# A selective scan on one core: two groups' products in one instruction, the third group's scan first, preparation one round sooner

## The chip, the core and the metric

The kernel runs on one core of a Trainium2 chip. A core has a matrix engine (TensorE, PE), a vector engine (VectorE, DVE), a scalar engine (ScalarE, ACT) and GpSimd (POOL), each with its own instruction stream in order; all DMAs of the stretch treated here are issued from the queue of a fifth, SyncE (SP). The metric is the device time of one execution in microseconds. The kernel before takes 8124.83 us, the median of three runs (8120.56 to 8125.09).

## The reference, cut to what matters

Four layers on an input of 4 x 56 x 56 x 96. Layers 0 and 1 each contain a selective scan over L = 3136 positions, in four directions, for each of four images, with 192 channels and 16 states per channel:

```python
d_a = jnp.exp(dt[..., None] * a)                # decay per position, channel, state
d_b = dt[..., None] * b_ssm[:, :, None, :]
def step(h, inp):
    da_t, db_t, x_t, c_t = inp
    h = da_t * h + db_t * x_t[..., None]        # the recurrence
    y_t = jnp.einsum('bds,bs->bd', h, c_t)      # sum over the states
    return (h, y_t)
```

dt is softplus of a projection of the input u, B and C are projections too. Around the scans stand normalisations, projections, small convolutions and gates; layers 2 and 3 are linear attention and a quantised feed-forward part. All of that runs beside the scans, in "lanes".

## The kernel before

**Tiling.** The scans of both layers are one stream of chunks: layer, image, direction, and within a direction 7 chunks of CS = 448 positions, 2 x 4 x 4 x 7 = 224 chunks. A chunk has two channel halves e of 96 channels, and four quarters q of the 16 states: 8 rounds a chunk, 1792 rounds in all. A round works on 128 partitions (32 channels x 4 states) and three groups g of channels (NG = 3), each of 448 positions in the free dimension.

**A round n** (loop of `scans`, lines 690 to 774):

- `products` (719): DVE writes du * B into the state tile h, for groups 0 and 1 in one instruction each; du (dt * u, spread over the partitions) is in SBUF, B in the PSUM tile b, which PE makes by a selecting matmul (`spread_b`, 616).
- `begin(n + 1)` (714): POOL makes the product of group 2 for the next round; [...] B comes from the SBUF tile cb.
- `scan` (726): DVE runs the recurrence over each group in place, groups 0, 1, 2, with the decay from the PSUM tiles da0, da1, da2. After each scan ACT makes the decay of the next round for that group (`decay`, 678), an exponential of dt. There is one da tile per group, so decay, scan and next decay follow each other.
- `kept` (696) and `carried` (691): ACT copies the last column of h to `carry` and the carry of an earlier chunk into the h of round n + 2. The tiles h come from a ring of 3.
- hc (768): POOL multiplies h of all three groups by C, in one instruction of 1344 elements; two rounds later PE sums it over the states (`add_up`, 799).

**Preparation of a chunk** happens in rounds o before its first one (o = 0): input columns U (479), a projection on PE (448), its split into high and low parts (609, 587), dt's projection and softplus (496, 506, 508), dt * u on POOL (`times_u`, 521, one instruction for both halves e), both parked in DRAM (`park`, 526) and read back spread over the partitions (`spread`, 532: dt and du, two buffers each), B and C fetched in the same way (`fetch`, 550: cb, five buffers). dtc and duc, the tiles before parking, have one buffer each.

**Lanes.** In two slots of each round ("F" before, "C" after the first scan) pieces of the other layers' work are put into the streams of PE, ACT, DVE and POOL, if a running account of ACT and PE time (`spend`, `room`) has room. Line 697 enters the scans' own ACT time by the number r of the round in the chunk. `keep_busy` fills PE with matmuls on zeros (786). The convolutions in lanes read windows of the input from tiles win (958), from a ring of NWIN = 5.

**Order.** PE, ACT, DVE and POOL run exactly in the order written. The order of SP's DMAs is made by the tile framework's scheduler. A DMA whose buffer isn't free yet, or whose source isn't written, waits at the head of SP's queue, and those behind it wait too.

Of the kernel before, what the change touches and what calls it, by code (L numbers as in the profile page):

```python
# [11 lines left out]
F32 = mybir.dt.float32  # L12
# [4 lines left out]
ALU = mybir.AluOpType  # L17
# [3 lines left out]
HS = 56  # L21
L = HS * HS
C = 96
DI = 192
NS = 16
NE = 2
NG = 3
NQ = 4
# [4 lines left out]
CS = 448  # L33
ROW = CS + 2
WIDE = NG * ROW + 2
# [1 line left out]
NCS = L // CS  # L37
RANK = (12, 6)
NW, LATE_NW = 13, 20
NWIN = 5  # L40
OWN = ()
OWN_TAIL = ()

SPARE = (0.9, 2.4)
ACT_LIMIT, PE_LIMIT = 4.0, 7.0
# [122 lines left out]
class Net:  # L168
    def __init__(self, ctx, tc, aps, at, out):
# [5 lines left out]
        self.dram = pool("dram", bufs=1, space=bass.MemoryType.DRAM)  # L175
        self.nw, self.nwin, self.depth, self.banks, self.ring = NW, NWIN, DEPTH, BANKS, None
        self.tables = False
# [334 lines left out]
        t = self.sp.tile([rows, 2 + n * CS], F32, name=name, bufs=bufs)  # L512
        return t[:, 2:].rearrange("p (n t) -> p n t", t=CS)

    def times_u(self, ch):

        ch.duc = self.sp.tile([C, NE, CS], F32, name="duc", bufs=1)
        u = self.both.rearrange("p e (h w) -> p e w h" if ch.orient else "p e (h w) -> p e h w", w=HS)
        lo = ch.c * CS // HS
        in_rows = lambda t: t.rearrange("p e (a b) -> p e a b", b=HS)  # L520
        self.nc.gpsimd.tensor_tensor(in_rows(ch.duc), in_rows(ch.dtc), u[:, :, lo : lo + CS // HS], ALU.mult)  # L521

    def park(self, t):
        d = self.dram.tile([NE, 32, NG, CS], F32, tag="dd", name="dd", bufs=6)
        for g in range(NG):
            self.nc.sync.dma_start(d[:, :, g].rearrange("e d t -> d e t"), t[32 * g : 32 * g + 32])
        return d

    def spread(self, t, d):
# [25 lines left out]
    def prepare(self, ch, o):  # L555

        nc = self.nc
        if o == -14:  # L560
            self.parameters(ch)
        if o == (-14 if ch.opening else -12):
            self.inputs(ch)
        if o == -9:
            ch.cd = self.dram.tile([2 * NS, CS], F32, tag="cd", name="cd", bufs=3)
            nc.sync.dma_start(ch.cd, ch.cf[: 2 * NS])
        elif o == -5:
            self.times_u(ch)
            ch.dtd = self.park(ch.dtc)
        elif o == -4:  # L570
            ch.dud = self.park(ch.duc)
            self.spread_dt(ch, 0)
        elif o == -3:
            self.spread_du(ch, 0)
        elif o == 0:
            self.spread_du(ch, 1)
            self.spread_dt(ch, 1)
        if -3 <= o <= 0:
            self.fetch(ch, o + 3)

    def prepare_on_scalar(self, ch, o):

        if o == -10:
            self.rows(ch)
        elif o in (-9, -8):
            part = slice(64 if o == -9 else 96, 128)
            self.nc.scalar.copy(ch.cf[part], ch.ps[part])  # L587
        elif o in (-7, -6):
            self.softplus(ch, o + 7)

    def on_tensor(self, ch, o):

        for e in self.projected(ch, o):
            self.project_step(ch, e)
        if o in (-10, -9):
            self.less(ch, 64 if o == -10 else 96)
        elif o in (-8, -7):
            self.step_size(ch, o + 8)

    def projected(self, ch, o):  # L600

        return () if o not in (-12, -11) else (o + 12,) if not ch.first else (0, 1) if o == -11 else ()

    def less(self, ch, at):

# [17 lines left out]
    def scans(self):  # L623
# [7 lines left out]
        nc, sp = self.nc, self.sp  # L631
        chunks = []
        for l in range(2):
            for i in range(NB):
                for n, (orient, rev) in enumerate(ORDER[l]):
                    for step in range(NCS):
                        ch = Step()
# [9 lines left out]
        rounds = [(ch, e, q) for ch in chunks for e in range(NE) for q in range(NQ)]  # L647
# [7 lines left out]
        def steps(n):  # L655

            return [(ch, n - per * j) for j, ch in enumerate(chunks[max(0, n // per) : n // per + 3], max(0, n // per))]

        def ahead(n):
            for ch, o in steps(n):  # L660
                self.on_tensor(ch, o)

        for n in range(-14, 0):
            for ch, o in steps(n):
                self.prepare(ch, o)
            if n > -8:
                yield "F", n, 0
            for ch, o in steps(n):
                self.prepare_on_scalar(ch, o)
            ahead(n)  # L670
            if n > -8:
                yield "C", n, 0

        def decay(n, g):

            if n < len(rounds):
                ch, e, q = rounds[n]
                nc.scalar.activation(da[g][:, INNER], ch.dt[e][:, g], AF.Exp, scale=ch.par.na[:, e, q, g : g + 1])  # L678

        def column(t, at):  # L680

            return t[:, at : at + 2 * ROW + 1 : ROW]

        def carried(n):

            if n < len(rounds):
                ch, e, q = rounds[n]
                hs[n] = sp.tile([128, WIDE], F32, name="h", bufs=3)
                if not ch.step:
                    return  # L690
                nc.scalar.copy(column(hs[n], ROW if ch.rev else 1), ch.par.carry[:, e, q])  # L691

        def kept(n):
            ch, e, q = rounds[n]
            if ch.step < NCS - 1:
                nc.scalar.copy(ch.par.carry[:, e, q], column(hs[n], 2 if ch.rev else CS + 1))  # L696

        def own(n):
            ch, e, q = rounds[n]
            return NQ * e + q in (OWN_TAIL if ch.l and ch.i else OWN)  # L700

        hs, bs = {}, {}

        def tokens(t):

            return self.groups(t, 2)[:, :, :CS]

        def begin(n):

            if n < len(rounds):  # L710
                ch, e, q = rounds[n]
                bs[n] = self.spread_b(ch, q)
                if not own(n):
                    nc.gpsimd.tensor_tensor(tokens(hs[n])[:, 2], ch.du[e][:, 2], ch.cb[q][:, 1], ALU.mult)  # L714

        def products(n):
            ch, e, q = rounds[n]
            for g in range(3 if own(n) else 2):
                nc.vector.tensor_tensor(tokens(hs[n])[:, g], ch.du[e][:, g], bs[n], ALU.mult)  # L719

        def scan(n, g):
            ch, e, q = rounds[n]
            c = 1 if ch.step else 0
            way = slice(CS + 1 + c, 1, -1) if ch.rev else slice(2 - c, CS + 2)
            h = hs[n][:, g * ROW :]
            nc.vector.tensor_tensor_scan(h[:, way], da[g][:, way], h[:, way], 0.0, ALU.mult, ALU.add)  # L726

        carried(0)
        carried(1)
        begin(0)  # L730
        self.exp_and_ln()
        self.tables = True
        for g in range(NG):
# [2 lines left out]
        for n, (ch, e, q) in enumerate(rounds):  # L736
            r = NQ * e + q
            products(n)
            for c, o in steps(n):
                self.prepare(c, o)  # L740
            self.half_round()
            strided = [1.5 + 1.5 * ch.orient] * (r % NQ == 2)
            strided += [1.5 + 1.5 * c.orient for c, o in steps(n) for _ in self.projected(c, o)]
            self.spend((0.6, 0.7, 1.7, 0, 0, 0, 0.7, 0.6)[r], (1.3, 1.3, 0, 0, 0, 0, 0.4, 0.4)[r] + sum(strided))
            yield "F", n, r
            for c, o in steps(n):
                self.prepare_on_scalar(c, o)
            ended = late.pop(0) if len(late) == 2 else None
            if ended:
                self.keep_busy(ended[2])  # L750
            begin(n + 1)
            if ended:
                self.add_up(*ended)
            ahead(n)
            self.half_round()
            for g in range(NG):
                if g == 1:
                    yield "C", n, r
                if g == 2 and ended and ended[2] == NQ - 1:
                    self.spend(0.6, 0)  # L760
                    self.keep_sums(*ended[:3])
                scan(n, g)
                if g == 2:
                    kept(n)
                decay(n + 1, g)
            carried(n + 2)
            hc = sp.tile([128, NG, CS], F32, name="hc", bufs=3)
            nc.gpsimd.tensor_tensor(  # L768
                hc, tokens(hs[n]), ch.cb[q][:, 0].unsqueeze(1).to_broadcast([128, NG, CS]), ALU.mult,
            )  # L770
            late.append((ch, e, q, hc))
            del hs[n], bs[n]
# [659 lines left out]
```

## Time and profile before

| | us |
|---|---|
| median of the runs | 8124.83 |
| the profiled execution: its time | 8113.91 |
| its span in the trace | 8112.0 |
| scans, first product to last hc | 88 to 7903 |
| DVE busy | 7522.7 |
| POOL busy | 7167.9 |
| PE busy, filler on zeros included | 7168.4 |
| ACT busy | 6094.8 |

The costliest groups of the page (line, engine, operation, output<-inputs, size, count | busy time, mean ns of one | idle time of the engine just before them, and what ended most of it):

```profile
L726 DVE TENSOR_TENSOR_SCAN h<-da,h 128x449 f32<-128x449 f32 (+1 forms) x5376 | 5505.1, 1071 | 101.0 <-ACT da L678 84.0
L768 POOL TENSOR_TENSOR hc<-h,cb 128x1344 f32<-128x1344 f32 x1792 | 4883.1, 2725 | 615.1 <-DVE h L726 490.0
L678 ACT ACTIVATE da<-dt,na 128x448 f32<-128x448 f32 x5376 | 3353.6, 632 | 1109.4 <-DVE h L726 1087.3
L719 DVE TENSOR_TENSOR h<-du,b 128x448 f32<-128x448 f32 x3584 | 2015.8, 603 | 132.5 <-PE b L616 86.3
L714 POOL TENSOR_TENSOR h<-du,cb 128x448 f32<-128x448 f32 x1792 | 1753.5, 979 | 54.4 <-ACT h L691 29.8
L521 POOL TENSOR_TENSOR duc<-dtc,U 96x896 f32<-96x896 f32 x224 | 482.9, 2156 | 34.6 <-ACT dtc L508 34.6
```

Busy time counts overlapping instructions once, so count times mean is a little more than busy time: an instruction of DVE starts while the one before it still finishes.

### The profile page before, as it was taken

Reading aid. Unit: us, or ns where it says so; the run is one execution under the profiler, and the core shown is the slowest. Engines: PE = TensorE matmul, PEld = TensorE weight load, DVE = VectorE, ACT = ScalarE, POOL = GpSimd, SP = SyncE. Lnnn points to the kernel's source line nnn. Section 1 sums busy time; section 2 is a strip of 40 time slices with the busy share of each in tenths; the row PEclk is TensorE's granted clock in tenths of the full one; section 3 lists DMA queues with packets and bytes.
Section 4 is the critical chain, followed back from the end, with each engine's and each line's share of the span. In section 5 each row is a group of like instructions: output and inputs, shape, how many; then the busy total and the mean of one; then the engine's idle time right before and its main releaser. Section 6 shows DMA issues by size and latency. Waiting matters only on the chain.

```text
span 8112.0 us, 112271 instructions
## 1 busy us (share of the span) xinstructions
PE 7168.4 (88%) x33189; PEld 2503.7 (31%) x33189; DVE 7522.7 (93%) x9600; ACT 6094.8 (75%) x12759; POOL 7167.9 (88%) x3989
## 2 busy tenths in 40 slices
PE   7889888889888988889889889998899988999887
PEld 3233233222332223322232223333233322433233
DVE  6999999999999999999999999999989999899982
ACT  6778878786778767886677866787767877678776
POOL 5999999999999999999989998899988999789980
PEclk8889989899998988999889998889988898898987
DMA  5555665567556666566555665555655556555552
GB/s 177 180 185 188 198 193 183 174 198 222 182 179 193 208 196 188 178 201 193 189 180 180 197 220 176 174 162 169 195 178 164 168 174 195 167 164 166 173 163 66
DMA packets 568235, 1467.46 MB, mean 181 GB/s; under 512 B 108034, under 2 KB 337156, under 8 KB 566756
## 3 DMA queue, kind: packets, MB, share of 16 engines
q1 hardware_dynamic: 566848, 1458.49, 57.3%
q8 instruction: 261, 4.28, 0.2%
q14 instruction: 354, 2.90, 0.1%
q10 hardware_dynamic: 772, 1.80, 0.1%
HBM read 1186.49 MB, written 273.47 MB: 180 GB/s over the span
## 4 chain that ended last, share of the span: by engine, by line
PE 34%; DVE 30%; ACT 16%; issue 12%; POOL 4%; DMA 2%; SPq 0%; DVEq 0%; POOLq 0%; ACTq 0%
DVE h L726 22%; PE y L799 7%; DVE h L719 7%; PE y L786 5%; ACT da L678 5%; PE y L795 4%; PE b L616 3%; POOL hc L768 2%; PE pp L496 2%; ACT L830 2%; PE pp L448 2%; PE ps L875 1%; PE ps L947 1%; PE ps L860 1%; ACT Y L806 1%
## 5 line engine op out<-in xcount | busy, mean ns | idle before, releaser
L726 DVE TENSOR_TENSOR_SCAN h<-da,h 128x449 f32<-128x449 f32 (+1 forms) x5376 | 5505.1, 1071 | 101.0 <-ACT da L678 84.0
L768 POOL TENSOR_TENSOR hc<-h,cb 128x1344 f32<-128x1344 f32 x1792 | 4883.1, 2725 | 615.1 <-DVE h L726 490.0
L678 ACT ACTIVATE da<-dt,na 128x448 f32<-128x448 f32 x5376 | 3353.6, 632 | 1109.4 <-DVE h L726 1087.3
L719 DVE TENSOR_TENSOR h<-du,b 128x448 f32<-128x448 f32 x3584 | 2015.8, 603 | 132.5 <-PE b L616 86.3
L799 PE MATMUL y<-hc,four 128*32 128x448 f32 x14336 | 1918.2, 610 | 18.8 <-POOL hc L768 18.5
L714 POOL TENSOR_TENSOR h<-du,cb 128x448 f32<-128x448 f32 x1792 | 1753.5, 979 | 54.4 <-ACT h L691 29.8
L786 PE MATMUL y<-w,zeros 128*96 128x448 bf16 x5067 | 1415.0, 398 | 0.0
L616 PE MATMUL b<-cf,sel 128*128 128x448 bf16 x1792 | 679.1, 379 | 667.5 <-DVE h L719 661.1
L786 PEld LDWEIGHTS <-zeros 128*96 128x96 bf16 x5067 | 629.3, 135 | 1168.5 <-issue 1011.7
L448 PE MATMUL pp<-U,wd 96*128 96x448 f32 x896 | 666.6, 833 | 14.2 <-DMA U<-u 4.5
L799 PEld LDWEIGHTS y<-hc,four 128*32 128x32 f32 x14336 | 294.8, 113 | 1198.6 <-issue 681.3
L795 PE MATMUL y<-Y,ident 96*96 96x448 f32 x672 | 542.1, 896 | 37.8 <-ACT Y L806 19.8
L496 PE MATMUL pp<-cf,wd 12*96 12x448 f32 (+1 forms) x896 | 484.8, 623 | 89.9 <-ACT dtc L506 55.8
L521 POOL TENSOR_TENSOR duc<-dtc,U 96x896 f32<-96x896 f32 x224 | 482.9, 2156 | 34.6 <-ACT dtc L508 34.6
L696 ACT COPY carry<-h 128x3 f32<-128x3 f32 x1536 | 302.0, 197 | 260.6 <-DVE h L726 254.6
L806 ACT COPY Y<-y 96x448 f32<-96x448 f32 x448 | 342.1, 764 | 29.7 <-PE y L799 28.5
L691 ACT COPY h<-carry 128x3 f32<-128x3 f32 x1536 | 280.0, 182 | 51.3 <-POOL hc L768 48.4
L587 ACT COPY cf<-pp 64x448 f32<-64x448 f32 x448 | 235.6, 526 | 81.0 <-PE pp L609 72.7
L506 ACT ACTIVATE dtc<-pp,wd 96x448 f32<-96x448 f32 x448 | 281.6, 629 | 18.5 <-PE pp L496 14.0
L616 PEld LDWEIGHTS <-sel 128*128 128x128 bf16 x1792 | 184.9, 103 | 349.2 <-issue 280.7
L860 PEld LDWEIGHTS ps<-avg,w 96*112 96x112 f32 (+2 forms) x1936 | 246.2, 191 | 94.7 <-issue 58.4
L875 PEld LDWEIGHTS ps<-ident,rs 112*96 112x96 f32 x1744 | 217.3, 187 | 131.4 <-issue 89.4
(381 smaller groups left out, 5597.3 us busy)
## 6 DMA issues: line engine op xcount, KB each, us to landing
cb<-cd SPq DMA_DIRECT2D x896, 448.0 KB, 4.8
dt<-dd SPq DMA_DIRECT2D x448, 672.0 KB, 5.6
du<-dd SPq DMA_DIRECT2D x448, 672.0 KB, 5.8
dd<-dtc SPq DMA_DIRECT2D x672, 112.0 KB, 2.0
dd<-duc SPq DMA_DIRECT2D x672, 112.0 KB, 2.0
win<-m SPq DMA_DIRECT2D x252, 112.0 KB, 4.4
U<-u SPq DMA_DIRECT2D x112, 168.0 KB, 4.6
w<-z SPq DMA_DIRECT2D x84, 224.0 KB, 4.3
```

The costliest lines, as they stand in the source:

```text
L448: self.nc.tensor.matmul(ch.ps.rearrange("p (a b) -> p a b", b=HS), ch.par.wx[:, e], self.in_order(self.U[e], ch.orient, ch.c * CS, CS), st ...
L496: self.nc.tensor.matmul(ch.pd, ch.par.wt[rows, C * e : C * e + C], ch.cf[rows], start=True, stop=True)
L521: self.nc.gpsimd.tensor_tensor(in_rows(ch.duc), in_rows(ch.dtc), u[:, :, lo : lo + CS // HS], ALU.mult)
L616: self.nc.tensor.matmul(ps, self.sel[:, q], self.upper(ch.cf), start=True, stop=True)
L678: nc.scalar.activation(da[g][:, INNER], ch.dt[e][:, g], AF.Exp, scale=ch.par.na[:, e, q, g : g + 1])
L714: nc.gpsimd.tensor_tensor(tokens(hs[n])[:, 2], ch.du[e][:, 2], ch.cb[q][:, 1], ALU.mult)
L719: nc.vector.tensor_tensor(tokens(hs[n])[:, g], ch.du[e][:, g], bs[n], ALU.mult)
L726: nc.vector.tensor_tensor_scan(h[:, way], da[g][:, way], h[:, way], 0.0, ALU.mult, ALU.add)
L768: nc.gpsimd.tensor_tensor(hc, tokens(hs[n]), ch.cb[q][:, 0].unsqueeze(1).to_broadcast([128, NG, CS]), ALU.mult,)
L786: self.nc.tensor.matmul(self.y[:C], self.zeros[:, :C], self.some, start=False, stop=False)
L795: nc.tensor.matmul(o, w, self.in_order(a, ch.orient, ch.c * CS, CS), start=True, stop=False)
L799: nc.tensor.matmul(self.y[32 * n : 32 * n + 32], self.four, hc[:, g], start=n == 3, stop=n == 3 or q == NQ - 1,)
```

## The change

- `products` is one instruction for groups 0 and 1, with b repeated by a stride of zero.
- The scans of a round run in the order 2, 0, 1.
- POOL's product of group 2 (now `third`) is made for round n + 2; the h ring has 4 tiles, and `carried` serves round n + 3.
- Preparation runs one round sooner throughout; `times_u` is one instruction per half e, in rounds -6 and -5, after `third` in POOL's stream; parking is one DMA per half and group (12 a chunk for 6).
- U of a later pass is loaded at o = -13, after that round's `times_u`, instead of at -12.
- The ring of windows has 4 tiles (NWIN). The options OWN and OWN_TAIL, empty before, are gone.

```diff
-NWIN = 5
+NWIN = 4
...
-    def times_u(self, ch):
+    def times_u(self, ch, e):
...
+        in_rows = lambda t: t[:, e].rearrange("p (a b) -> p a b", b=HS)
+        u = self.in_order(self.U[e], ch.orient, ch.c * CS, CS)
+        self.nc.gpsimd.tensor_tensor(in_rows(ch.duc), in_rows(ch.dtc), u, ALU.mult)
...
-            self.nc.sync.dma_start(d[:, :, g].rearrange("e d t -> d e t"), t[32 * g : 32 * g + 32])
+            self.nc.sync.dma_start(d[e, :, g], t[32 * g : 32 * g + 32, e])
...
-        if o == -9:
+        elif o == -10:
             ch.cd = self.dram.tile([2 * NS, CS], F32, tag="cd", name="cd", bufs=3)
             nc.sync.dma_start(ch.cd, ch.cf[: 2 * NS])
+        elif o == -6:
+            ch.dtd = self.park(ch.dtc, 0)
+            self.park(ch.dtc, 1, ch.dtd)
         elif o == -5:
-            self.times_u(ch)
-            ch.dtd = self.park(ch.dtc)
+            ch.dud = self.park(ch.duc, 0)
+            self.spread_dt(ch, 0)
         elif o == -4:
-            ch.dud = self.park(ch.duc)
-            self.spread_dt(ch, 0)
-        elif o == -3:
+            self.park(ch.duc, 1, ch.dud)
             self.spread_du(ch, 0)
         elif o == 0:
             self.spread_du(ch, 1)
             self.spread_dt(ch, 1)
-        if -3 <= o <= 0:
-            self.fetch(ch, o + 3)
+        if -4 <= o < 0:
+            self.fetch(ch, o + 4)
...
+        def u_products(n):
+            for ch, o in steps(n):
+                self.prepare_on_gpsimd(ch, o)
+            for ch, o in steps(n):
+                if o == -13 and not ch.opening:
+                    self.inputs(ch)
...
-                hs[n] = sp.tile([128, WIDE], F32, name="h", bufs=3)
+                hs[n] = sp.tile([128, WIDE], F32, name="h", bufs=4)
...
+        def third(n):
+
+            if n < len(rounds):
+                ch, e, q = rounds[n]
+                nc.gpsimd.tensor_tensor(tokens(hs[n])[:, 2], ch.du[e][:, 2], ch.cb[q][:, 1], ALU.mult)
 
         def products(n):
             ch, e, q = rounds[n]
-            for g in range(3 if own(n) else 2):
-                nc.vector.tensor_tensor(tokens(hs[n])[:, g], ch.du[e][:, g], bs[n], ALU.mult)
+            b = bs[n].unsqueeze(1).to_broadcast([128, 2, CS])
+            nc.vector.tensor_tensor(tokens(hs[n])[:, :2], ch.du[e][:, :2], b, ALU.mult)
...
             begin(n + 1)
+            third(n + 2)
+            u_products(n)
...
-            for g in range(NG):
-                if g == 1:
+            for at, g in enumerate((2, 0, 1)):
+                if at == 1:
                     yield "C", n, r
...
-            carried(n + 2)
+            carried(n + 3)
```

More of the change, by code (lines that the diff above doesn't have):

```diff
@@ L39 @@
 NW, LATE_NW = 13, 20
-NWIN = 5
-OWN = ()
-OWN_TAIL = ()
+NWIN = 4
 SPARE = (0.9, 2.4)
@@ L513, in shifted, with park @@
         return t[:, 2:].rearrange("p (n t) -> p n t", t=CS)
-    def times_u(self, ch):
[L517 to L524, printed above, removed]
+    def times_u(self, ch, e):
+        if e == 0:
+            ch.duc = self.sp.tile([C, NE, CS], F32, name="duc", bufs=1)
+        in_rows = lambda t: t[:, e].rearrange("p (a b) -> p a b", b=HS)
+        u = self.in_order(self.U[e], ch.orient, ch.c * CS, CS)
+        self.nc.gpsimd.tensor_tensor(in_rows(ch.duc), in_rows(ch.dtc), u, ALU.mult)
+    def park(self, t, e, d=None):
+        if e == 0:
+            d = self.dram.tile([NE, 32, NG, CS], F32, tag="dd", name="dd", bufs=6)
         for g in range(NG):
-            self.nc.sync.dma_start(d[:, :, g].rearrange("e d t -> d e t"), t[32 * g : 32 * g + 32])
+            self.nc.sync.dma_start(d[e, :, g], t[32 * g : 32 * g + 32, e])
         return d
@@ L559, in prepare @@
         nc = self.nc
-        if o == -14:
+        if o == -15:
             self.parameters(ch)
-        if o == (-14 if ch.opening else -12):
-            self.inputs(ch)
-        if o == -9:
+            if ch.opening:
+                self.inputs(ch)
+        elif o == -10:
             ch.cd = self.dram.tile([2 * NS, CS], F32, tag="cd", name="cd", bufs=3)
             nc.sync.dma_start(ch.cd, ch.cf[: 2 * NS])
+        elif o == -6:
+            ch.dtd = self.park(ch.dtc, 0)
+            self.park(ch.dtc, 1, ch.dtd)
         elif o == -5:
-            self.times_u(ch)
-            ch.dtd = self.park(ch.dtc)
+            ch.dud = self.park(ch.duc, 0)
+            self.spread_dt(ch, 0)
         elif o == -4:
-            ch.dud = self.park(ch.duc)
-            self.spread_dt(ch, 0)
-        elif o == -3:
+            self.park(ch.duc, 1, ch.dud)
             self.spread_du(ch, 0)
@@ L577, in prepare, with prepare_on_gpsimd @@
             self.spread_dt(ch, 1)
-        if -3 <= o <= 0:
-            self.fetch(ch, o + 3)
+        if -4 <= o < 0:
+            self.fetch(ch, o + 4)
     def prepare_on_scalar(self, ch, o):
-        if o == -10:
+        if o == -11:
             self.rows(ch)
-        elif o in (-9, -8):
-            part = slice(64 if o == -9 else 96, 128)
+        elif o in (-10, -9):
+            part = slice(64 if o == -10 else 96, 128)
             self.nc.scalar.copy(ch.cf[part], ch.ps[part])
-        elif o in (-7, -6):
-            self.softplus(ch, o + 7)
+        elif o in (-8, -7):
+            self.softplus(ch, o + 8)
+    def prepare_on_gpsimd(self, ch, o):
+        if o in (-6, -5):
+            self.times_u(ch, o + 6)
     def on_tensor(self, ch, o):
@@ L594, in on_tensor @@
             self.project_step(ch, e)
[L595 to L598, printed above, removed]
+        if o in (-11, -10):
+            self.less(ch, 64 if o == -11 else 96)
+        elif o in (-9, -8):
+            self.step_size(ch, o + 9)
     def projected(self, ch, o):
-        return () if o not in (-12, -11) else (o + 12,) if not ch.first else (0, 1) if o == -11 else ()
+        return () if o not in (-13, -12) else (o + 13,) if not ch.first else (0, 1) if o == -12 else ()
     def less(self, ch, at):
@@ L657, in steps @@
             return [(ch, n - per * j) for j, ch in enumerate(chunks[max(0, n // per) : n // per + 3], max(0, n // per))]
+        def u_products(n):
[3 more added lines that the diff above has]
+                if o == -13 and not ch.opening:
+                    self.inputs(ch)
         def ahead(n):
@@ L661, in ahead @@
                 self.on_tensor(ch, o)
-        for n in range(-14, 0):
+        for n in range(-15, 0):
             for ch, o in steps(n):
@@ L696, in kept @@
                 nc.scalar.copy(ch.par.carry[:, e, q], column(hs[n], 2 if ch.rev else CS + 1))
-        def own(n):
-            ch, e, q = rounds[n]
-            return NQ * e + q in (OWN_TAIL if ch.l and ch.i else OWN)
         hs, bs = {}, {}
@@ L712, in begin @@
                 bs[n] = self.spread_b(ch, q)
-                if not own(n):
-                    nc.gpsimd.tensor_tensor(tokens(hs[n])[:, 2], ch.du[e][:, 2], ch.cb[q][:, 1], ALU.mult)
+        def third(n):
+            if n < len(rounds):
+                ch, e, q = rounds[n]
+                nc.gpsimd.tensor_tensor(tokens(hs[n])[:, 2], ch.du[e][:, 2], ch.cb[q][:, 1], ALU.mult)
         def products(n):
             ch, e, q = rounds[n]
-            for g in range(3 if own(n) else 2):
-                nc.vector.tensor_tensor(tokens(hs[n])[:, g], ch.du[e][:, g], bs[n], ALU.mult)
+            b = bs[n].unsqueeze(1).to_broadcast([128, 2, CS])
+            nc.vector.tensor_tensor(tokens(hs[n])[:, :2], ch.du[e][:, :2], b, ALU.mult)
         def scan(n, g):
@@ L726, in scan @@
             nc.vector.tensor_tensor_scan(h[:, way], da[g][:, way], h[:, way], 0.0, ALU.mult, ALU.add)
-        carried(0)
-        carried(1)
+        for n in range(NG):
+            carried(n)
         begin(0)
+        third(0)
+        third(1)
         self.exp_and_ln()
@@ L751, in scans @@
             begin(n + 1)
+            third(n + 2)
+            u_products(n)
             if ended:
@@ L755, in scans @@
             self.half_round()
-            for g in range(NG):
-                if g == 1:
+            for at, g in enumerate((2, 0, 1)):
+                if at == 1:
                     yield "C", n, r
-                if g == 2 and ended and ended[2] == NQ - 1:
+                if at == 2 and ended and ended[2] == NQ - 1:
                     self.spend(0.6, 0)
@@ L762, in scans @@
                 scan(n, g)
-                if g == 2:
+                if at == 2:
                     kept(n)
                 decay(n + 1, g)
-            carried(n + 2)
+            carried(n + 3)
             hc = sp.tile([128, NG, CS], F32, name="hc", bufs=3)
```

## The prediction

> **What bounds the kernel now.** I read the busy shares first, then the stretch of the scans alone, then the vector engine (DVE) in order of time, then its waits, then GpSimd (POOL) in order of time and the waits of the DMA queue (SP).
>
> The page's busy line and the scan stretch (columns of the second: stretch, length, then each engine's busy time and instructions, granted clock, DMA share, GB/s):
>
> ```profile
> PE 7168.4 (88%) x33189; PEld 2503.7 (31%) x33189; DVE 7522.7 (93%) x9600; ACT 6094.8 (75%) x12759; POOL 7167.9 (88%) x3989
> ...
> 88.00:7903.00 7815.00, 6940.13 (x32496) 2399.83 (x32496) 7446.10 (x9394) 5915.64 (x12424) 7136.68 (x3953) 0.90 0.59 184
> ```
>
> 1792 rounds take 7815 us, 4.36 us each. DVE is idle for 7815 - 7446 = 369 us of it. PE's share holds 1415 us of filler (line 786, zeros), so PE is less full than it looks. POOL is the close second: 7137 us.
>
> DVE in order of time, where no other work is mixed in (start, length, engine, line):
>
> ```profile
> 2070.12 1.12 DVE L719 TENSOR_TENSOR h<-du,b 128x448 f32<-128x448 f32 x2
> 2071.16 3.05 DVE L726 TENSOR_TENSOR_SCAN h<-da,h 128x449 f32<-128x449 f32 x3
> 2074.13 1.12 DVE L719 TENSOR_TENSOR h<-du,b 128x448 f32<-128x448 f32 x2
> 2075.18 3.05 DVE L726 TENSOR_TENSOR_SCAN h<-da,h 128x449 f32<-128x449 f32 x3
> 2078.14 1.12 DVE L719 TENSOR_TENSOR h<-du,b 128x448 f32<-128x448 f32 x2
> ```
>
> From start to start: two products 1.04 to 1.05 us, three scans 2.96 to 2.97, a round 4.01 without a gap. Counting round lengths in these DVE rows over the whole trace, 1130 of 1792 rounds are below 4.05 us: in almost two thirds DVE alone sets the pace. The others hold either work of the side lanes on DVE (some 450 instructions, about 220 us) or a wait. The waits of DVE in the scan stretch (us in total, times, longest):
>
> ```profile
> DVE h L719 <- PE b L616: 86.3, 94, 9.5
> DVE h L726 <- ACT da L678: 84.0, 167, 2.5
> DVE w L889 <- PE ps L875: 33.5, 19, 3.7
> ...
> DVE h L726 <- POOL h L714: 15.1, 15, 2.0
> ```
>
> They are scattered over PE, ACT and side lanes; POOL's product of the third group ends last only 15 times.
>
> POOL in order of time around the product dt*u (line 521):
>
> ```profile
> 3011.14 2.73 POOL L768 TENSOR_TENSOR hc<-h,cb 128x1344 f32<-128x1344 f32 x1 [4.70 <-DVE h L726]
> 3013.81 1.77 POOL L521 TENSOR_TENSOR duc<-dtc,U 96x896 f32<-96x896 f32 x1
> 3015.54 0.98 POOL L714 TENSOR_TENSOR h<-du,cb 128x448 f32<-128x448 f32 x1
> 3016.48 2.74 POOL L768 TENSOR_TENSOR hc<-h,cb 128x1344 f32<-128x1344 f32 x1
> 3019.17 0.98 POOL L714 TENSOR_TENSOR h<-du,cb 128x448 f32<-128x448 f32 x1
> 3020.10 2.74 POOL L768 TENSOR_TENSOR hc<-h,cb 128x1344 f32<-128x1344 f32 x1
> ```
>
> hc and the third product take 3.62 us a round (3016.48 to 3020.10), and every eighth round line 521 adds 1.73 us (1.76 to 2.59 long, by orientation). 8 x 3.62 + 2.15 = 31.1 us a chunk, against 8 x 4.01 = 32.1 on DVE.
>
> [...] the trace has 0.52 from product to product, [...] The trace's own check: a 97x97 product of the same kind (line 1330) lasts 230 ns and a 448 one 603, so 1.06 ns per element and about 0.13 us fixed, of which 0.08 overlaps the next instruction. The forecast goes by the trace's 0.52, [...]
>
> **The change part by part.**
>
> *Joint product.* Two instructions of 448 become one of 896 with b repeated. Estimate: [...], against 1.05: 0.057 us a round, 1792 x 0.057 = 102 us. No DVE row has a repeated PSUM operand. Bounds: 0.97 at best (saves 0.08, 143 us), 1.05 at worst (saves nothing); not longer, since the elements are the same. I take 0.99. Not all of it arrives: the waits view has some 430 waits, so about a quarter of the rounds end on PE, ACT or a lane; half of those I count as lost, leaving 88%: **-90 us**.
>
> *Scan of group 2 first.* Without it the scan of group 0 would follow directly on the joint product that feeds it. With it, a scan of 0.99 us stands between. Scan, decay on ACT and next scan of a group stay one round apart, with the same 2.4 us to spare (4.01 - 0.99 - 0.63). Zero.
>
> *Third product two rounds ahead, four h buffers.* Before, POOL has it done 3.6 us after the end of the previous round's scans, and it is needed at 7.0: 3.4 us to spare, 1.2 in the round with line 521. After, it is needed at 4 + 4 + 1.0 = 9.0: 5.4 to spare. The 15.1 us of waits for it nearly go: **-12 us**. What is late next on POOL is hc: its h buffer must be free before ACT copies the carry in at the round's end, hc ends 2.7 us into the round, so 1.3 us are to spare there, as before; the longer h ring moves carry and buffer together.
>
> *dt*u in halves over two rounds.* 448 instructions for 224. From POOL's rows, (2725 - 978) / 896 = 1.95 ns per element, so about 0.1 us fixed: 224 x 0.09 = 20 us more POOL time. It hides in POOL's idle time before hc (490 us on line 726), but that shrinks: +5 us. In return the lump behind which hc waits is about 1.1 us twice instead of 2.2 once.
>
> *Preparation a round sooner.* On PE and ACT it is the same work one round earlier. The table of ACT time kept free for it (by round number) is not moved, so lanes are put where softplus is: +5 us (0 to 15).
>
> *SP's queue.* Parking dt and dt*u now takes 12 DMAs a chunk instead of 6: 1344 more at 0.42 us of issue (1.26 for three), 560 us. The bytes stay. SP has that time:
>
> ```profile
> SPq L550 <- POOL hc L768: 1401.2, 598, 7.8
> SPq L526 <- ACT dtc L508: 1256.8, 209, 19.9
> SPq L526 <- POOL duc L521: 928.6, 217, 8.7
> ```
>
> But with five cb buffers, fetch of quarter q=1..3 a round sooner takes a buffer whose last reader, hc four rounds back, ends only 2.7 us into the issuing round. The POOL instruction that needs it comes two hc later, at least 7.2 us; landing is 4.8 (page's DMA part) and issue 0.4: 2.0 us to spare, where it was about 6. Zero, if nothing else blocks the queue.
>
> *U of the next pass* (seven times): loaded after the last half of dt*u, which ends 0.7 us into the next round, in which PE already wants it 2.8 us in; landing is 4.6 us. PE stands about 3 us; half reaches DVE: +10 us (0 to 28).
>
> *Four win buffers.* The third window of a convolution now takes the buffer that PE has just read; at the head of each of four images it is needed a round later, landing 4.4 plus issue 1.3: PE 2 to 3 us late: +8 us (0 to 13).
>
> *Opening.* One more round of prologue and every opening load a round sooner: +4 us (0 to 20).
>
> Sum: -90 - 12 + 5 + 5 + 10 + 8 + 4 = **-70 us**. The profiled execution has 8113.9 us (span 8112.0), so 8044; the median of the runs shown, 8124.8, lies 10.9 above it: **8055 us**, 0.86% faster. Range of this case: 8010 to 8095.
>
> **The rivals.**
>
> *POOL becomes the bound.* A vertical chunk needs 8 x 3.62 + 2.6 + 0.1 = 31.7 us there, DVE then 8 x 3.955 = 31.6. For it: the tie, and hc already starts late after line 521. Against: lanes and waits give DVE another 0.2 us a round. If half of the 90 us is lost, 8100.
>
> *The joint product saves nothing* (1.05 us): -12 + 32 remains, 8145. Against it speaks that the fixed part shows in every DVE row.
>
> *SP's queue makes it slower.* A fetch with 2.0 us to spare stands in one queue with stores that wait for ACT or DVE up to 10 us (the Y stores, line 811, 348 us in 59 waits). Where one is over 2 us late, POOL stops before the third product, and POOL has nearly no free time, so that time counts in full. It outweighs the gain from 70/224 = 0.3 us per chunk; at 0.7 us per chunk +157 - 70 gives 8210. Against: SP waits 2.3 us on average in front of fetches, so it is early, not late.
>
> **How the numbers follow.** Main case 0.62 (8055), POOL bound 0.13 (8100), nothing saved 0.07 (8145), SP queue 0.18 (8210). 0.2% is 16 us, about what a measurement can tell from no change. Faster: main case and three quarters of POOL, 0.70; slower: SP queue mostly and half of "nothing saved", 0.20; same 0.10. Low end: joint product at its best and all of it arriving, 8113.9 - 143 + 11 = 7982, little likely, so 7995; high end to the SP case: 8170.
>
> **What would show it.** Right: one DVE product a round with about 1.07 us length, the next scan 0.99 us after its start; undisturbed rounds at 3.95; no wait of a scan for POOL; hc waits for DVE fall clearly below 490 us. SP rival: POOL's third product waits for cb or du DMAs (17.4 us before) in the hundreds. POOL rival: ACT's copy of the carry waits for hc far above 48 us. The forecast is wrong if undisturbed rounds stay at 4.01, or if they reach 3.95 and DVE's idle time grows by over 70 us.

## The result: 0.5% slower, with the mechanism forecast in place

The changed kernel takes 8159.29 us (median, 8156.76 to 8169.87) against 8122.69 us before; the ratio is 1.0051, 95% interval 1.0033 to 1.0068. The forecast was 8055 us; the time lies inside the range given, but on the other side of no change. The profiled execution has 8156.8 us, span 8155.0, where before it had 8113.9 and 8112.0: 43 us more. Below, times of different runs are compared by their ratio to the kernel before, which ran beside each of them.

DVE in order of time, changed kernel (start, length, engine, line):

```profile
2102.02 1.06 DVE L732 TENSOR_TENSOR h<-du,b 128x896 f32<-128x896 f32 x1
2102.99 3.05 DVE L739 TENSOR_TENSOR_SCAN h<-da,h 128x449 f32<-128x449 f32 x3
2105.96 1.06 DVE L732 TENSOR_TENSOR h<-du,b 128x896 f32<-128x896 f32 x1
2106.94 3.05 DVE L739 TENSOR_TENSOR_SCAN h<-da,h 128x449 f32<-128x449 f32 x3
```

The joint product takes 0.98 us from its start to the scan's; an undisturbed round takes 3.94 to 3.95 us, against 4.01. That is what the forecast rested on. The stretch of the scans, and DVE's longest waits in it:

```profile
88.00:7938.00 7850.00, 6888.50 (x32415) 2377.43 (x32414) 7335.25 (x7596) 5903.99 (x12412) 7158.66 (x4173) 0.90 0.57 183
```

```profile
DVE h L739 <- ACT da L691: 171.5, 216, 3.1
DVE h L732 <- PE b L621: 142.3, 130, 13.1
DVE w L1099 <- PE ps L1097: 41.6, 19, 3.6
...
DVE h L739 <- POOL h L727: 1.0, 2, 0.5
```

DVE works 7335 us instead of 7446: 111 us saved. But it is idle 7850 - 7335 = 515 us instead of 369, 146 more. Waits for ACT's decay doubled (84.0 to 171.5), those for PE's b rose from 86.3 to 142.3, and a lane's step on line 1099 appears (41.6). The wait for POOL's third product is gone, as forecast.

Where the idle time lies is told by the round within the chunk (idle time ahead of DVE's instructions, summed from the trace over all chunks with the shortest gaps too, so a little above the 369 and 515; us):

| round r | 0 | 1 | 2 | 3 | 4 | 5 | 6 | 7 | sum |
|---|---|---|---|---|---|---|---|---|---|
| before | 66 | 30 | 47 | 82 | 67 | 7 | 22 | 56 | 377 |
| changed | 99 | 73 | 73 | 33 | 65 | 24 | 120 | 38 | 525 |

Round 3, where the double product dt*u used to stand in POOL's stream, became better by 49 us. Round 6 became worse by 98, rounds 0 to 2 together by 102. In those rounds ACT's preparation now stands: its first copy of the projection moved from round 6 to round 5, softplus from rounds 1 and 2 to 0 and 1. The copy of the finished sums (line 823) stays in rounds 1 and 5. And the table on line 759 (697 before), from which the lanes learn how much ACT time to leave free, still has 0 for round 5 and 0.7 for round 1, where the 1.6 us end of softplus now runs.

One such place, round 718 (r = 6): ACT, PE and DVE in order of time, changed kernel.

```profile
3200.92 1.28 ACT L921 ACT_TABLE_LOAD   x1
3202.22 0.64 ACT L921 ACTIVATE w<-ps,inb 128x448 f32<-128x448 f32 x1
3202.88 0.63 ACT L922 ACTIVATE w<-ps,inb 64x448 f32<-64x448 f32 x1
3203.51 1.28 ACT L847 ACT_TABLE_LOAD   x1
...
3205.31 0.63 ACT L487 ACTIVATE cf<-pp,cscale 128x448 f32<-128x448 f32 x1
3205.84 1.19 ACT L691 ACTIVATE da<-dt,na 128x448 f32<-128x448 f32 x2
3206.96 0.52 ACT L823 COPY Y<-y 96x448 f32<-96x448 f32 x1
```

```profile
3206.00 0.53 PE L614 MATMUL pp<-cf,minus 64*64 64x448 bf16 x1 [4.17 <-ACT cf L487]
3206.45 4.32 PE L1097 MATMUL ps<-w,w 128*96 128x448 f32 x6
```

```profile
3206.57 1.09 DVE L739 TENSOR_TENSOR_SCAN h<-da,h 128x449 f32<-128x449 f32 x1 [2.10 <-ACT da L691]
3210.82 0.68 DVE L1099 SCALAR_TENSOR_TENSOR w<-ps,c,w 96x448 f32<-96x448 f32 x1 [3.15 <-PE ps L1097]
```

A lane's piece with two table loads (ACT_TABLE_LOAD, 1.28 us each; 3.83 us of work from 3200.92 on) stands ahead of the copy cf (487) and of the decays. PE, in order, waits 4.17 us for cf; the lane's matmuls behind it come late; DVE waits 2.10 us for its decay and then 3.15 us for the lane's sum. One overfull round of ACT costs DVE 5.25 us.

This is one of the worst places, and the chunk being prepared opens a direction, which puts two more short instructions of ACT in the rows left out. But it is of the common kind. By a count in the traces, table loads start during round 5 in 37 of the 224 chunks, in both kernels. In the rounds that follow them (r = 6) DVE is idle for 10 us in the kernel before, and for 80 of round 6's 120 us in the changed one.

### The profile page after: what moved, and what is told of

The parts are those of the page before. It is cut to its first block, busy times and chain, and to the rows that moved or that the text cites. A ratio compares the mean times of both kernels' runs of the same rounds, so it can differ in the third digit from the quotient of the medians.

```text
span 8155.0 us, 110085 instructions
## 1 busy us (share of the span) xinstructions
PE 7126.6 (87%) x33155; PEld 2487.4 (31%) x33155; DVE 7421.3 (91%) x7811; ACT 6089.5 (75%) x12757; POOL 7198.6 (88%) x4213
## 4 chain that ended last, share of the span: by engine, by line
PE 30%; DVE 29%; ACT 16%; issue 15%; POOL 6%; DMA 4%; SPq 1%; DVEq 0%; POOLq 0%; ACTq 0%
DVE h L739 19%; DVE h L732 9%; PE y L816 6%; ACT da L691 4%; POOL hc L785 4%; PE y L803 3%; PE y L812 3%; PE pp L446 2%; PE pp L494 2%; ACT L847 2%; PE ps L877 2%; PE ps L892 2%; PE b L621 1%; PE ps L964 1%; DMA cb<-cd 1%
## 5 line engine op out<-in xcount | busy, mean ns | idle before, releaser
L739 DVE TENSOR_TENSOR_SCAN h<-da,h 128x449 f32<-128x449 f32 (+1 forms) x5376 | 5504.9, 1072 | 182.0 <-ACT da L691 171.5
L732 DVE TENSOR_TENSOR h<-du,b 128x896 f32<-128x896 f32 x1792 | 1904.4, 1063 | 144.5 <-PE b L621 142.3
L519 POOL TENSOR_TENSOR duc<-dtc,U 96x448 f32<-96x448 f32 x448 | 526.3, 1175 | 23.4 <-ACT dtc L506 23.4
L494 PE MATMUL pp<-cf,wd 12*96 12x448 f32 (+1 forms) x896 | 467.3, 602 | 68.8 <-ACT cf L587 37.9
L614 PE MATMUL pp<-cf,minus 64*64 64x448 bf16 x448 | 178.2, 398 | 144.5 <-ACT cf L487 82.5
```

The source lines that it names most:

```text
L494: self.nc.tensor.matmul(ch.pd, ch.par.wt[rows, C * e : C * e + C], ch.cf[rows], start=True, stop=True)
L732: nc.vector.tensor_tensor(tokens(hs[n])[:, :2], ch.du[e][:, :2], b, ALU.mult)
```

## The experiments

Three theories stood at first. 1: preparation meets the turnover of the sums (the rounds in which finished sums are copied out), with a table that doesn't know. 2: DVE's gain can't arrive, since PE, ACT or POOL are at their own limit. 3: POOL is late and holds ACT's carry.

### Preparation on ACT and PE back in its old rounds

```diff
-        if o == -11:
+        if o == -10:
             self.rows(ch)
-        elif o in (-10, -9):
+        elif o in (-9, -8):
...
-        elif o in (-8, -7):
-            self.softplus(ch, o + 8)
+        elif o in (-7, -6):
+            self.softplus(ch, o + 7)
...
-        elif o == -6:
+        elif o == -5:
             ch.dtd = self.park(ch.dtc, 0)
             self.park(ch.dtc, 1, ch.dtd)
-        elif o == -5:
             ch.dud = self.park(ch.duc, 0)
-            self.spread_dt(ch, 0)
```

(projection, split, step size, parameters and B, C to DRAM one round later too; dt spread at -4)

> The changed kernel, but ScalarE's and TensorE's part of the preparation (projection, its split, softplus) back in the rounds where the kernel before has it; dt*u stays in halves in rounds -6 and -5, the third product two rounds ahead. Theory 1 (the new waits come from preparation now meeting the turnover of the sums on ACT and PE, in rounds 1, 2, 5 and 6 of a chunk): idle time of DVE falls back to about 370 us and the 111 us of DVE time arrive, 8010 to 8060 us. Theory 2 (DVE's gain can't arrive, because PE, ACT or POOL are at their own limit): still 8110 or more, DVE idle above 450 us. Theory 3 (POOL late: hc, carry, next third product): about 8130, since POOL's order is as in the changed kernel.

Ratio 0.9968 (0.9957 to 0.9978): 0.83% below the changed kernel, of the sign that theory 1 expects, above its window. Round 6 falls back to 38 us of DVE's idle time, the sum is 477. The halves of dt*u now directly follow softplus, and POOL waits for it (one of these waits, of 26.2 us, lies outside the scans' steady part):

```profile
POOL duc L519 <- ACT dtc L506: 109.8, 53, 26.2
```

Round 3 has 102 us idle. So this run doesn't separate theory 1 cleanly; it put a wait of its own in.

### The joint product split again, in the changed kernel

```diff
-            b = bs[n].unsqueeze(1).to_broadcast([128, 2, CS])
-            nc.vector.tensor_tensor(tokens(hs[n])[:, :2], ch.du[e][:, :2], b, ALU.mult)
+            for g in range(2):
+                nc.vector.tensor_tensor(tokens(hs[n])[:, g], ch.du[e][:, g], bs[n], ALU.mult)
```

> The changed kernel with the joint product split again into two instructions of 448. Theory 1: the waits are new and apart from DVE's pace, so the 0.06 us a round come back nearly in full, 8235 to 8270 us. Theory 2: DVE's idle time takes most of it, 8160 to 8190, idle falling by 80 us or more. Theory 3: in between, since POOL gets 0.06 us a round more to catch up.

Ratio 1.0135 (1.012 to 1.015). Against 1.0051 the joint product is worth 0.84%, 68 us of the 111. The time lies between the windows of theories 1 and 2, and DVE's idle time is only about 35 us lower than with the joint product, so both have a part: three fifths arrive, and without the joint product the change would have cost 1.35%.

### The joint product alone, in the kernel before

```diff
-            for g in range(3 if own(n) else 2):
-                nc.vector.tensor_tensor(tokens(hs[n])[:, g], ch.du[e][:, g], bs[n], ALU.mult)
+            b = bs[n].unsqueeze(1).to_broadcast([128, 2, CS])
+            nc.vector.tensor_tensor(tokens(hs[n])[:, :2], ch.du[e][:, :2], b, ALU.mult)
```

> The kernel before with the joint product alone; scans stay in the order 0, 1, 2, so the scan of group 0 follows on the product that feeds it. If the order 2, 0, 1 matters, that scan starts only when the product is complete, about 0.1 us later than in the changed kernel (1.06 against 0.98), and the round stays at 4.01 to 4.05: 8110 to 8150. If it doesn't, undisturbed rounds fall to 3.95, and by theory 1 and 3 (preparation and POOL as before) the time is 8020 to 8050, by theory 2 8100 or more.

Ratio 1.0178 (1.0161 to 1.0195), slower than the case in which the order matters. DVE in order of time:

```profile
2092.48 1.06 DVE L719 TENSOR_TENSOR h<-du,b 128x896 f32<-128x896 f32 x1
2093.64 3.06 DVE L726 TENSOR_TENSOR_SCAN h<-da,h 128x449 f32<-128x449 f32 x3
2096.62 1.06 DVE L719 TENSOR_TENSOR h<-du,b 128x896 f32<-128x896 f32 x1
```

The scan that needs the product starts 1.16 us after it, not 0.98: 0.18 us a round, and the round is 4.14 us. It is so in all 1792 rounds: 1.156 us at the least, where the changed kernel has under 1.1 us in 1540. The order 2, 0, 1 is what makes the joint product pay, by far more than the forecast's "zero" suggests for it taken by itself.

### The tables moved with the preparation

```diff
-SPARE = (0.9, 2.4)
+SPARE = (0.95, 2.4)
...
-            self.spend((0.6, 0.7, 1.7, 0, 0, 0, 0.7, 0.6)[r], (1.3, 1.3, 0, 0, 0, 0, 0.4, 0.4)[r] + sum(strided))
+            self.spend((0.7, 1.7, 0, 0, 0, 0.7, 0.6, 0.6)[r], (1.3, 0, 0, 0, 0, 0.4, 0.4, 1.3)[r] + sum(strided))
```

> The changed kernel with the tables of ScalarE and TensorE time set aside by round number moved one round sooner, like the preparation itself; the spare time per half round is 0.95 instead of 0.9, without which the lanes don't end in time. Theory 1, if the stale table is the cause: DVE's waits for ACT in rounds 1, 2 and 6 fall and the time is 8070 to 8120. Theory 1, if the work itself collides there: 8140 to 8170. Theories 2 and 3: 8150 to 8170.

SPARE is the time of ACT and of PE, in us, by which the account's backlog falls each half round; a lane's piece goes in only if the backlog with it stays under a limit (ACT_LIMIT, PE_LIMIT).

Ratio 0.9914 (0.9895 to 0.9933), 8046.22 us: faster than both kernels, and better than expected. Waits of DVE in this run:

```profile
DVE h L732 <- PE b L621: 130.8, 102, 12.1
DVE h L739 <- ACT da L691: 126.5, 206, 3.7
```

DVE's idle time sums to 418 us instead of 525, and round 6 to 27 instead of 120; round 2 falls from 73 to 56, but round 1 rises from 73 to 81, against the expectation. Table loads start during round 5 in 12 chunks instead of 37, and DVE is idle for 9 us behind them instead of 80. The step on line 1099 is no longer among its longest waits. The spare time was changed with the tables, so it needed runs of its own.

### Is it the spare time?

```diff
-SPARE = (0.9, 2.4)
+SPARE = (0.95, 2.4)
```

in the changed kernel and in the kernel before:

> The changed kernel with only the spare time per half round at 0.95 instead of 0.9; the tables stay where they are. If the tables made the gain of the run that moved them, 8140 to 8170 us. If the spare time did (lanes end sooner, or stand elsewhere), 8040 to 8060, like that run.

> The kernel before with the spare time at 0.95. If the tables are the cause, 8105 to 8135, no change. If the spare time is worth 1% by itself, 8020 to 8050.

1.0102 (1.0078 to 1.0126) and 1.0036 (1.002 to 1.0052). More spare time costs 0.4 to 0.5% in both; that it lets lanes into rounds that are full is argued, not shown. So the moved tables gain 1.9% at equal spare time.

These sizes have a rival that no run held fixed, TensorE's granted clock. Within the kernels, over all 250 recorded executions, one whose mean clock is 0.001 lower is 4.3 us longer (a straight-line fit, give or take 0.6). The means of the two runs with 0.95 are 0.890 and 0.893, beside 0.898 for the kernel before; the run with the moved tables has 0.8995, beside 0.8967. With the clock's share taken out by that fit, an estimate, spare time of 0.95 costs 6 us in the changed kernel and 10 us in the kernel before, and the moved tables gain 1.3% instead of 1.9%. Whether a table lowers the clock by where it puts the lanes, or the clock differs for another reason, is open. The idle times by round don't depend on this fit.

The other way to make room for them, spare time 0.9 and ACT's limit at 4.4:

```diff
-ACT_LIMIT, PE_LIMIT = 4.0, 7.0
+ACT_LIMIT, PE_LIMIT = 4.4, 7.0
```

> The changed kernel with both tables moved one round sooner, spare time 0.9 as it was, and ScalarE's limit at 4.4 instead of 4.0, the other way to let the lanes end in time. If the tables are the cause: 8040 to 8090, and DVE's idle time in round 6 of a chunk below 60 us, against 120. If it was the spare time: 8140 or more.

0.9978 (0.9969 to 0.9987), 0.73% below the changed kernel, with round 6 at 22 us. The 8080.93 us lie in the window, but the kernel before took only 8097 beside this run; by the ratio the gain falls short of it. It has the same sign at about half the size; a limit of 4.4 was not run with the old tables, so how much the limit itself costs is open.

### POOL relieved

```diff
-        self.nc.gpsimd.tensor_tensor(in_rows(ch.duc), in_rows(ch.dtc), u, ALU.mult)
+        self.nc.gpsimd.tensor_tensor(in_rows(ch.duc)[:, :1], in_rows(ch.dtc)[:, :1], u[:, :1], ALU.mult)
```

> The changed kernel with dt*u made for the first of 8 rows only, the rest of the tile stays zero (that part of the computation is left out): POOL loses some 450 us of work, its order and all waits stay. Theory 3 (POOL late) and the rival that POOL is the bound: 8050 to 8090 and the carry's wait for hc near zero. Tables as the cause: 8130 to 8165.

POOL's busy time falls from 7198.6 to 6839.3 us, and the ratio is 1.006 (1.0038 to 1.0081), no better than the changed kernel's 1.0051. ACT's waits of the carry for hc, in the kernel before, the changed kernel and this run:

```profile
ACT h L691 <- POOL hc L768: 48.4, 64, 2.8
ACT h L704 <- POOL hc L785: 120.5, 90, 4.4
ACT h L707 <- POOL hc L788: 54.9, 34, 5.3
```

They rise with the change and fall by more than half here, not to near zero, and nothing is gained. So theory 3 and the rival "POOL becomes the bound" fall as the main cause.

### Which table, which entry

TensorE's table alone (spare time 0.9), ScalarE's alone (0.95), and both at 0.98 (the edit shown is the first):

```diff
-            self.spend((0.6, 0.7, 1.7, 0, 0, 0, 0.7, 0.6)[r], (1.3, 1.3, 0, 0, 0, 0, 0.4, 0.4)[r] + sum(strided))
+            self.spend((0.6, 0.7, 1.7, 0, 0, 0, 0.7, 0.6)[r], (1.3, 0, 0, 0, 0, 0.4, 0.4, 1.3)[r] + sum(strided))
```

> The changed kernel with only TensorE's table moved one round sooner, spare time 0.9 as it was. If ScalarE's table is what matters (round 1 now holds softplus of 1.6 us under an entry of 0.7), no gain: 8140 to 8175. If TensorE's matters: 8060 to 8110.

> The changed kernel with only ScalarE's table moved, spare time 0.95 (needed for the lanes to end). If ScalarE's table is the cause: 8030 to 8080, against 8176 with that spare time and the old tables. If TensorE's: 8150 or more.

> Both tables moved, spare time 0.98 instead of 0.95: how far the time depends on where the lanes happen to fall. If the tables carry the gain, 8030 to 8090 again. If the one good time was a lucky placement, 8100 or more.

1.0031 (1.0021 to 1.0042), 0.9937 (0.9919 to 0.9955), 0.9929 (0.9911 to 0.9947). ScalarE's table carries it, 1.65% at equal spare time; TensorE's is worth 0.2%. The run at 0.98 speaks against one lucky placement of the lanes as the cause. At equal clock, by the fit above (0.895 for ScalarE's alone, beside 0.8972), ScalarE's table is worth some 1.4%.

In ScalarE's table the first copy's entry, 0.7 us from round 6 to 5, and softplus' entries, from rounds 1 and 2 to 0 and 1, each alone (below the table of the first edit; the second has 0.7, 1.7, 0, 0, 0, 0, 0.7, 0.6):

```diff
-            self.spend((0.6, 0.7, 1.7, 0, 0, 0, 0.7, 0.6)[r],
+            self.spend((0.6, 0.7, 1.7, 0, 0, 0.7, 0, 0.6)[r],
```

> The changed kernel with spare time 0.95 and one entry of ScalarE's table moved: the 0.7 us for the first copy of the projection from round 6 to round 5, where that copy now runs beside the copy of the sums. If this round is where the time goes (DVE's idle time in round 6 of a chunk), 8060 to 8110, against 8176 with the old table. If the softplus entries carry it, 8150 or more.

> The changed kernel with spare time 0.95 and only softplus' entries of ScalarE's table moved, from rounds 1 and 2 to rounds 0 and 1. If softplus under a lane's work is where the time goes, 8060 to 8110. If round 5 carries it, 8140 to 8180, and DVE's idle time in round 6 stays near 120 us.

1.0022 (1.0014 to 1.0029) and 1.0019 (1.0004 to 1.0034), from 1.0102. Each is worth 0.8% by the ratios, so neither alone is "the" entry. That the two add up to the whole 1.65% should not be leaned on: at equal clock (0.891 and 0.8994, beside 0.8973) they come to some 0.6 and 0.25%, of 1.4. Nor do the two edits make up the whole table: the first leaves 0 for round 6, where a copy of the split stands (line 587), and the second reserves 0.6 us a chunk less. Yet they work in different places: with the entry of round 5 DVE's idle time in round 6 falls to 36 us, and the lanes that move into round 6 (1.08 us of ACT a round, 0.42 with the old table, counted as below) are followed by 107 us in round 7; with softplus' entries round 6 stays at 98. ACT's time for lanes and table loads in round 5, summed from the trace over rounds 224 to 1119, fits this: 1.32 us a round in the changed kernel (1.02 with spare time 0.95), 0.47 with the entry of round 5, 1.20 with softplus' entries.

### A stale table in the kernel before

The moved tables in the kernel before, whose preparation hasn't moved, spare time 0.95:

> The kernel before, whose preparation stands where its tables say, with the tables moved one round sooner, so that they are stale in the other direction; spare time 0.95. If a stale table costs time by itself: 8170 to 8230, against 8129 with that spare time and its own tables. If it only matters beside a faster DVE: 8110 to 8140.

0.9994 (0.9985 to 1.0003), against 1.0036 with its own tables and that spare time. The expectation failed: tables that are one round early cost nothing here, they gain 0.42%. So as much of the 1.9% that they gain in the changed kernel need not come of the old tables being stale; the moved ones may simply place the lanes better. What is left, about 1.5%, goes with a reservation one round late. I read the difference so: the account is a backlog that drains at 1.9 us a round at most, so an early entry keeps lanes out ahead of the work, and a late one only after it. That reading is argued, not shown.

### What the joint product is worth with the tables moved

The split product in the run with both tables moved:

> Both tables moved, spare time 0.95, and the joint product split again: what the joint product is worth where the account fits. If the waits of the stale table had swallowed part of its 111 us, it now arrives nearly in full: 8140 to 8160, against 8046 with the joint product. If PE, ACT and POOL take their share in any case, as with the old tables (68 us of 111): 8105 to 8125.

0.9987 (0.998 to 0.9995), against 0.9914: 0.73%, 59 us of 111. The expectation that a fitting table would let nearly all of it through failed; 374 us idle become 418 with the joint product. At equal clock, by the fit above, this value and the 68 us with the old tables both come out near 50 us. The part that doesn't arrive goes to DVE's waits for other engines with either table, as theory 2 says; they are many, and no run names a single one.

## Why the prediction was wrong

The prediction named its own sign of being wrong: undisturbed rounds at 3.95 us and DVE's idle time up by over 70 us. That is what came, with 146 us more.

- **The step that failed** is "Preparation a round sooner": "The table of ACT time kept free for it (by round number) is not moved, so lanes are put where softplus is: +5 us (0 to 15)". The mechanism was named and its size guessed without a count. Moving ScalarE's table gained 1.65% at spare time 0.95 (1.0102 to 0.9937), some 134 us; both tables, at spare time 0.9 with the limit raised, 0.73%, some 59 us. Even the lower value, less the 0.42% (34 us) that the moved tables gain in the kernel before, leaves some 25 us, above the range given. And the loss is not only where softplus is: in round 5 the copy of the projection meets the copy of the sums, and round 6 alone lost 98 us of DVE's time. The size of one collision could be read beforehand: the code counts 3.8 us of ACT for the lane's piece with two table loads, DVE has 2.4 us to spare for its decay, and PE waits in order behind the preparation's copy.
- **The share of the gain that arrives** was put at 88% of 102 us. The saving itself was right, 111 us; but 68 us arrive (59 with the tables moved), 53 to 61%, or near 45% at equal clock. Counting waits and losing half of those rounds was too kind: the waits grow when DVE is faster (374 to 418 us with the tables moved). Forecast and result lie 107 us apart; these two terms can make up that much, but how it is split between them the runs don't fix.
- **Joint product**: 0.99 forecast, 0.98 measured, no price for the repeated operand. Right; but the 0.99, and with it the 0.057 us a round and the 102 us, was my estimate, which no trace of the kernel before showed.
- **Scan order**: "zero" was right for the change as a whole; the cost it avoids, 0.18 us a round, was not priced.
- **Third product two rounds ahead**: DVE's waits for it fell from 15.1 to 1.0 us. Right.
- **dt*u in halves**: 526.3 us of POOL against 482.9, +43 instead of +20, and hc's waits for DVE stayed at 491 instead of falling; POOL's added work is not what costs the time, as the relieved run shows.
- **SP's queue**: the DMAs' waits grew in front of fetches (1401.2 to 2006.5 us for hc), but POOL waits for cb 16.8 us, 17.4 before. The rival named for a slower kernel was the wrong one.
- **U, windows, opening**: PE's waits for U rose from 6.4 to 18.7 us, for windows from 2.4 to 21.6; the first product starts 2.8 us later and the first 40 rounds have 8 us more idle. How much of it reaches DVE was not measured apart.

With the tables moved the kernel runs at 0.9914 of before, which is the ratio forecast for the change without them; that agreement is partly luck, since too much gain and too little cost cancel in it.

## What to carry to other kernels

When a stage is moved in a software pipeline, every table that is keyed by its position should move with it; here reservations one round late cost far more than reservations one round early. Price a moved stage by what it meets in its new round (here the copy of the sums), not by its own length. Merging two instructions paid here only with independent work between the merged one and its reader.

## What the runs showed of the hardware

In the joint-only run the scan that reads the joint product starts 1.16 us after the product's start (1.156 at the least): the product's length of 1.06 us and 0.10 more. In the changed kernel, where the scan behind the product is of another group, it starts after 0.98. So to need its predecessor's result costs that scan 0.18 us a round here; what these 0.18 us consist of, no run shows.
